# Graph layer plus masked attention in fp32: who makes the operand sums of the last two output projections, and when

## The chip, the cores and the metric

The kernel runs on one core of a Trainium2 chip. The metric is the device time of one execution in microseconds (us). A core has a matrix engine (TensorE, PE in the profile; its weight loads are PEld), VectorE (DVE), ScalarE (ACT), GpSimd (POOL) and SyncE (SP), whose queue issues DMA transfers. Each engine works through its own queue in program order and waits for the others through semaphores.

## The reference

Input x is 64 batches of 256 nodes with 512 features, with one 256x256 weighted adjacency for all of them. Two layers follow each other, each with a residual:

```python
h = relu(layernorm(x))
x = x + einsum('nm,bmd->bnd', adj, h) @ weight + bias
h = relu(layernorm(x))
q, k, v = h @ Wq + bq, h @ Wk + bk, h @ Wv + bv          # 8 heads of 64
scores = q @ k.T / 8 + (1 - adj) * -1e9                  # per head
x = x + softmax(scores) @ v  @ Wo + bo
```

All of it is fp32.

## The kernel before

**Groups.** The 64 batches are taken two at a time: 32 groups, g = 0 to 31 (`NG` = 32). Layer 0 runs over all groups first and leaves its results in DRAM; layer 1 then runs group after group. The output of the kernel is complete when the last group's output projection is added to its residual and sent out. Everything that the change touches lies in groups 30 and 31, so at the very end of the program.

**Projections with seven products.** A 512x512 projection (q, k, v, o) is split into halves in both directions and computed with seven products in place of eight (Strassen's scheme, in Winograd's form). That takes sums of weight blocks (`s1` to `s4`, made once) and sums of operand blocks, made for each group by `Halves.sums`, line 446: t1 = b12 - b11, t2 = b22 - t1, t3 = b22 - b12, t4 = b21 - t2. Each is one elementwise subtraction of 128x512. For the output projection the operand is `oT`, and its sums appear as `t_o` in the profile.

From group 2 on (`FIRST2`), `project2` splits three of the seven products once more. Their operand sums are made by `Blocks.sums` (lines 537 to 539), called through `block_outputs`: first from `oT` (tile `rest` for groups below 31, `t2o` for group 31), then from t4 (tile `t24o`).

`project2` is a generator with seven steps, written here with the tiles of the output projection of group g:

1. a11 x b11 into bank `o_ga`, added into the residual x
2. s3 x t3 into bank `o_gc`, added
3. s2 x t2 into `o_ga` again, added
4. the first small products of the three inner splits (one 128x128 product each), and `o_gb`
5. s1 x t1 into `o_ga`, added
6. the second small products of the inner splits (twelve matmul instructions), with six VectorE adds of 128x128
7. the rest: small products into `o_gc`, `o_ga`, the three third ones, the last adds, and the output DMA

Since `o_ga` is accumulated over several steps and read in between, step 3 waits until VectorE has added step 1's result, and step 5 until it has added step 3's. Both banks are seeded with the bias by ScalarE (`seeded`, line 255) before step 1.

**Attention.** A group's eight heads go in two halves, qd = 0 and 1. `score` computes the scores on TensorE (`sc`, 32 matmuls), VectorE scales and masks them (line 904), GpSimd subtracts a per-column maximum (line 910), ScalarE takes the exponential (line 915), and GpSimd adds the two key tiles (line 922, tile `as`). In group 31 the third of the four subtractions (by its place in the call order) is put on VectorE instead (line 908). `attend` multiplies `as` with ones for the denominators (`pden`) and the exponentials with v (`pav`), ScalarE copies the denominators out (line 947), VectorE inverts them (line 951, four pieces of 128x128; two of these before the next scores, two after, but all four at once for the last attention), and `divide` multiplies `pav` with the inverses into `oT` (line 969). Then it calls `note` (line 963: ScalarE sums the inverses into `stats`, for the overflow flag) and the operand sums described above.

**Order.** The program is written out by hand: the order in which Python issues the instructions is their order on each engine. `after(n, fn)` puts a call off by n ticks; `run(gen, n)` takes n steps of a generator, with a tick after each. So the engine that a sum runs on, and the tick at which it is issued, decide what stands before and behind it in a queue.

**Around the change.** For groups 30 and 31 the sums of `oT` are issued on VectorE, right inside `divide`. In group 31 the sums of the inner splits are on VectorE too, and `note` is called at once. After the scores of (31, 1), five steps of group 30's output projection run, then the last attention, then a tick (which brings its `divide`), then steps 6 and 7 of group 30, then six steps of group 31's projection, then the flag (lines 1078 to 1082: compare, reduce, a 1x1 matmul `pf`, copy), and step 7.

PSUM has eight banks, given out first-in first-out by `bank` and `give`. By that order, `o_30a` and `o_30c` are seeded into the banks that the third and the fourth VectorE mask operation (line 904) of the scores (31, 1) have emptied.

Of the kernel before, what the change touches and what calls it, by code (L numbers as in the profile page):

```python
# [198 lines left out]
def kernel(  # L199
# [16 lines left out]
    nc = tc.nc  # L216
# [7 lines left out]
    NG = B // GB  # L224
# [23 lines left out]
    def bank(shape, name, seed=None):  # L248

        i = next(i for i in free_banks if seed is None or whole[i])  # L250
        free_banks.remove(i)
        t = psum.tile(shape, F32, tag=f"bank{i}", name=name)
        bank_of[id(t)] = (i, t)
        if seed is not None:
            nc.scalar.copy(t, seed[:, None, :].to_broadcast(shape))
        return t

    def give(t, all_written=True):
        i = bank_of.pop(id(t))[0]
        free_banks.append(i)  # L260
        whole[i] = all_written
# [5 lines left out]
    def after(delay, fn, *args):  # L267
        entered[0] += 1
        later.append((clock[0] + delay, entered[0], fn, args))

    def tick():
        clock[0] += 1
        due = sorted((e for e in later if e[0] <= clock[0]), key=lambda e: e[:2])
        later[:] = [e for e in later if e[0] > clock[0]]
        for _, _, fn, args in due:
            fn(*args)
# [152 lines left out]
    class Halves:  # L429
# [12 lines left out]
        def sums(self, eng, which=("t1", "t2", "t3", "t4"), c=slice(0, 2)):  # L442
            args = {"t1": ("b12", "b11"), "t2": ("b22", "t1"), "t3": ("b22", "b12"), "t4": ("b21", "t2")}
            for n in which:
                p, q = args[n]
                eng.tensor_tensor(self.t[n][:, c, :], self.operand(p, c), self.operand(q, c), op=ALU.subtract)  # L446
# [61 lines left out]
    FIRST2 = 2  # L508
# [269 lines left out]
    H1T, HH, HO = {}, {}, {}  # L778

    def load_hidden(g):  # L780
        H1T[g] = xpool.tile([P, GB, DC, N], F32, tag="x", name=f"h1T_{g}")
        for k in range(GB):
            nc.sync.dma_start(H1T[g][:, k].rearrange("p d n -> p (d n)").rearrange("p (i n) -> p i n", n=N // NI),
                              HT[g][:, :, :, k, :].rearrange("p d i n -> p (d i) n"))

    def load_residual(g):
        X[g] = xpool.tile([P, T, D], F32, tag="x", name=f"x1_{g}")
        nc.sync.dma_start(X[g], X1[g].rearrange("k (t p) d -> p (k t) d", p=P))

    def hidden_sums(g, *steps):  # L790

        HH[g] = Halves(f"h_{g}", [H1T[g][:, k] for k in range(GB)], 0 if g else 1)
        for step, n in zip(steps, ("t3", "t1", "t2", "t4")):
            after(step, HH[g].sums, nc.gpsimd, (n,))
# [10 lines left out]
    def block_outputs(g, eng, step):  # L805
        x = OT[g][:, 2:4, :].rearrange("p c (k n j) -> p k c n j", k=GB, j=P)
        if g < NG - 1:
            t4 = act.tile([P, 4, P], F32, tag="t24o", name=f"t24o_{g}")
            t = AS["rest"][:, 2:4, :].rearrange("p k (q j) -> p k q j", j=P)
        else:  # L810
            t4 = act.tile([P, 4, P], F32, tag="t24", name=f"t24o_{g}")
            t = act.tile([P, GB, 4, P], F32, tag="t2", name=f"t2o_{g}")
        O2[g] = block_sums_of(x, t, HO[g], t4, eng, step)

    def block_sums_of(x, t, halves, t4, eng, step):
        both = Blocks(x, t)
        last = Blocks(halves.t["t4"].rearrange("p c (n j) -> p c n j", j=P), t4)
        after(step, both.sums, eng)
        after(step + 1, last.sums, eng)
        return {"b21": Blocks(x[:, 0], t[:, 0]), "b22": Blocks(x[:, 1], t[:, 1]), "t4": last}  # L820
# [40 lines left out]
    def seed_outputs(g):  # L861
        return seeded(L1["o"][1], f"o_{g}")
# [61 lines left out]
    def attend(g, qd):  # L924


        pd = bank([P, GN], f"pden_{g}_{qd}")
        po = [bank([P, GN], f"pav_{g}_{qd}_{f}") for f in range(2)]
        for b in range(GB):
            for h in range(4):  # L930
                nc.tensor.matmul(pd[h * 32:(h + 1) * 32, b * N:(b + 1) * N], ones[:, 0:32], AS[h // 2, b][:, h % 2, :],  # L931
                                 start=(b == 0), stop=True, tile_position=(0, h * 32), skip_group_check=True)
        for b in range(GB):
            v = V[g][qd, b]
            for k in range(NT):
                for f in range(2):
                    for h in range(4):
                        nc.tensor.matmul(po[f][h * 32:(h + 1) * 32, b * N:(b + 1) * N],  # L938
                                         v[:, k, h * HD + f * 32:h * HD + f * 32 + 32],
                                         A[h // 2, b][:, (h % 2) * NT + k, :],  # L940
                                         start=(b + k == 0), stop=(k == NT - 1), tile_position=(0, h * 32),
                                         skip_group_check=True)
        i = g * HQ + qd
        if i == 0:
            AS["rest"] = act.tile([P, 4, GN], F32, tag="yT1", name="rest")
        den, rden = AS["rest"][:, 0, :], AS["rest"][:, 1, :]
        nc.scalar.activation(den, pd, AF.Identity, accum_out=stats[:, 0, i:i + 1])  # L947
        give(pd)

        def invert(c):  # L950
            nc.vector.reciprocal(rden[:, c * P:(c + 1) * P], den[:, c * P:(c + 1) * P])  # L951

        early = 2 if g >= FIRST2 and (g, qd) != (NG - 1, 1) else 4
        for c in range(early):
            invert(c)
        if qd == 0:

            last = g == NG - 1
            OT[g] = (xpool if last else act).tile([P, DC, GN], F32, tag="x" if last else "r", name=f"oT_{g}")
            HO[g] = Halves(f"o_{g}", [OT[g][:, :, k * N:(k + 1) * N] for k in range(GB)], 0 if last else 1)  # L960

        def note():
            nc.scalar.activation(den, rden, AF.Identity, accum_out=stats[:, 1, i:i + 1])

        def divide():
            for c in range(early, 4):
                invert(c)
            for f in range(2):
                nc.vector.tensor_tensor(OT[g][:, 2 * qd + f, :], po[f], rden, op=ALU.mult)
                give(po[f])  # L970
            if g < NG - 1:
                after(3, note)
            else:
                note()
            eng = nc.gpsimd if g < NG - 2 else nc.vector
            if qd == 0:
                HO[g].sums(eng, ("t1",))
            else:
                HO[g].sums(eng, ("t3", "t2", "t4"))
                if g >= FIRST2:  # L980
                    block_outputs(g, eng if g == NG - 1 else nc.gpsimd, 8 if g == NG - 2 else 2)

        after(1, divide)

    def run(gen, steps=99):

        for _ in zip(range(steps), gen):
            tick()
# [50 lines left out]
    for g in range(NG):  # L1039
        attend(g, 0)  # L1040
        load_residual(g)
        if g + 2 < NG:
            load_hidden(g + 2)
        score(g, 1, 5 if g < NG - 1 else 3)
        tick()
        if g == 0:
            for n, tag in ((4 * DC, "w0_sb"), (4, "w0_s1"), (4, "w0_s2"), (4, "w0_s4"), (4, "adjT"), (4, "b0_r")):
                t = const.tile([P, n, P], F32, tag=tag, name=f"spare_{tag}")
                spare.extend(t[:, i, :] for i in range(n))
        for n, at in (("q", 7),) if g == 0 else (("k", 1), ("v", 5)) if g == 1 else (("o", 2),) if g == 2 else ():  # L1050
            for i, work in enumerate(block_sums(n)):
                after(at + i // 3, *work)
        if g + 1 < NG:
            run(queries_keys(g + 1))
        else:
            last = post(g - 1, seed_outputs(g - 1))
            run(last, 5)
        attend(g, 1)
        if g + 1 < NG:
            score(g + 1, 0, 5)  # L1060
            tick()
            steps = values(g + 1)
            run(steps, 5)
            seeds = seed_outputs(g) if g + 2 < NG else None
            run(steps)
            if g + 2 < NG:
                hidden_sums(g + 2, 2, 3, 4, 5)
                if g + 2 >= FIRST2:
                    block_hidden(g + 2, 6)
                run(post(g, seeds))  # L1070
    tick()
    run(last)
    last = post(NG - 1, seed_outputs(NG - 1))
    run(last, 6)

    bad = tmp.tile([P, 2 * NG * HQ], F32, tag="u", name="bad")
    worst = small.tile([P, 1], F32, tag="worst", name="worst", bufs=1)
# [41 lines left out]
```

## Time and profile before

| what | value |
|---|---|
| median of 8 runs | 2678.29 us (2676.13 to 2680.62) |
| the profiled execution | 2680.57 us, of which the span is 2678.7 us |
| PE, PEld busy in the span | 2646.5 us (99%), 2281.4 us (85%) |
| DVE, ACT, POOL busy | 1860.0 us (69%), 965.5 us (36%), 1779.5 us (66%) |
| scores of (31, 1) start on PE | 2623.12 us |
| output projection of group 30 starts | 2632.26 us |
| last attention (`pden`) starts | 2643.32 us |
| output projection of group 31 starts | 2654.43 us |
| last PE and last DVE instruction end | 2671.8 and 2672.3 us |

The profiled execution is one run, 2.3 us above the median. Times inside it count from the span's start. The table of windows gives, for each stretch, its length, the busy time of PE, PEld, DVE, ACT and POOL with the number of instructions, the mean TensorE clock as a share of the full one, the DMA share and GB/s. The timeline lists start, duration, engine, line, output and inputs, and in square brackets how long the engine had been idle and whose work ended that.

### The profile page before, as it was taken

To read this page: it belongs to the slowest core of one execution; us is meant where nothing else is said; L and a number is where in the kernel's file an instruction comes from. 1 tells how busy PE (TensorE), PEld (TensorE's weight loads), DVE (VectorE), ACT (ScalarE), POOL (GpSimd) and SP (SyncE) were. 2 spreads that over 40 slices of the span, in tenths; PEclk is the share of its full clock that TensorE was granted. 3 is DMA by queue.
4 is the path that set the end of the run, shared out by engine and by line. 5 is a ranking of instruction groups with operands and counts; after the bars stand their busy time and mean duration, and the time that the engine had idled before them with its cause. 6 is when DMAs were issued, how large, how long until landed. Compare 5 with 4: busy or idle time off the path is not lost.

```text
span 2678.7 us, 50183 instructions
## 1 busy us (share of the span) xinstructions
PE 2646.5 (99%) x19332; PEld 2281.4 (85%) x19332; DVE 1860.0 (69%) x4103; ACT 965.5 (36%) x1875; POOL 1779.5 (66%) x1568
## 2 busy tenths in 40 slices
PE   8999999999999999999999999999999999999997
PEld 7888888888888888888888888888888888888885
DVE  7777777774467666667676666676766666667676
ACT  4444445453333333333333333333333333333331
POOL 3454544444778777777777777777777777777772
PEclk9999999999999999999999999999999999999998
DMA  7776666663122211111111111122221111111110
GB/s 185 185 198 168 157 171 165 171 160 80 47 64 57 55 48 48 48 48 48 48 49 48 48 48 48 48 56 65 65 54 48 48 48 48 49 48 48 48 48 33
DMA packets 281058, 210.93 MB, mean 79 GB/s; under 512 B 145904, under 2 KB 212976, under 8 KB 280816
## 3 DMA queue, kind: packets, MB, share of 16 engines
q1 hardware_dynamic: 280352, 207.15, 29.8%
q8 instruction: 155, 2.54, 0.4%
q14 instruction: 87, 0.71, 0.1%
q10 hardware_dynamic: 464, 0.52, 0.1%
HBM read 106.96 MB, written 100.66 MB: 78 GB/s over the span
## 4 chain that ended last, share of the span: by engine, by line
PE 97%; DVE 2%; DMA 0%; ACT 0%; issue 0%; POOL 0%; ACTq 0%; DVEq 0%
PE sc L898 9%; PE pav L938 8%; PE py L714 8%; PE q L564 3%; PE k L564 3%; PE v L564 3%; PE o L564 3%; PE pden L931 2%; DVE a L904 0%; DVE x L665 0%; PE o_30a L453 0%; PE w_1a L453 0%; PE v_1a L453 0%; PE q_1a L453 0%; PE w_31a L453 0%; PE w_22a L453 0%
## 5 line engine op out<-in xcount | busy, mean ns | idle before, releaser
L910 POOL TENSOR_TENSOR a<-a,top 128x1024 f32<-128x1024 f32 x254 | 592.5, 2366 | 493.9 <-DVE a L904 493.9
L904 DVE SCALAR_TENSOR_TENSOR a<-sc,maskT 128x512 f32<-128x512 f32 x512 | 312.0, 682 | 121.9 <-PE sc L898 121.9
L922 POOL TENSOR_TENSOR as<-a 128x512 f32<-128x512 f32 x256 | 318.9, 1278 | 9.1 <-ACT a L915 8.0
L915 ACT ACTIVATE a<-a 128x1024 f32<-128x1024 f32 x256 | 270.6, 1058 | 10.2 <-POOL a L910 7.8
L53 POOL TENSOR_TENSOR rs<-rs,mhalf 128x2 f32<-128x2 f32 (+1 forms) x97 | 77.9, 803 | 267.6 <-DVE nb L52 267.5
L951 DVE RECIPROCAL rest<-rest 128x128 f32<-128x128 f32 x256 | 224.5, 920 | 34.4 <-ACT rest L947 34.4
L898 PE MATMUL sc<-q,k 64*128 64x256 f32 x2048 | 238.4, 382 | 0.0
L938 PE MATMUL pav<-a,v 128*32 128x256 f32 x4096 | 233.6, 379 | 0.0
L898 PEld LDWEIGHTS sc<-q,k 64*128 64x128 f32 x2048 | 194.2, 187 | 44.7 <-issue 26.3
L714 PE MATMUL py<-adjT,h 128*128 128x256 f32 x1024 | 228.6, 382 | 0.9 <-DVE adjT L333 0.9
L714 PEld LDWEIGHTS py<-adjT,h 128*128 128x128 f32 x1024 | 196.0, 192 | 28.6 <-ACT h L693 1.2
L938 PEld LDWEIGHTS pav<-a,v 128*32 128x32 f32 x4096 | 133.4, 110 | 87.9
L741 ACT ACTIVATE h<-x,nb,rs 128x512 f32<-128x512 f32 x128 | 97.1, 806 | 307.1 <-POOL nb L54 307.1
L947 ACT ACTIVATE rest<-pden 128x512 f32<-128x512 f32 x64 | 38.3, 598 | 414.7 <-PE pden L931 414.7
L665 DVE TENSOR_TENSOR k<-k,k 128x128 f32<-128x128 f32 (+1 forms) x300 | 96.2, 353 | 126.0 <-PE k L564 124.0
L446 POOL TENSOR_TENSOR t_y<-yT 128x256 f32<-128x256 f32 (+1 forms) x96 | 87.5, 912 | 46.0 <-ACT yT L724 42.5
L665 DVE TENSOR_TENSOR x<-o,x 128x128 f32<-128x128 f32 (+1 forms) x360 | 111.1, 350 | 3.1
L665 DVE TENSOR_TENSOR q<-q,q 128x128 f32<-128x128 f32 (+1 forms) x300 | 96.1, 353 | 13.5 <-PE q L564 11.4
L665 DVE TENSOR_TENSOR v<-v,v 128x128 f32<-128x128 f32 (+1 forms) x300 | 95.4, 352 | 14.5 <-PE v L564 11.4
L761 DVE BATCH_NORM_STATS2 st<-x 128x6 f32<-128x256 f32 x256 | 96.4, 419 | 4.4
L693 ACT ACTIVATE h<-x,nb,rs 128x512 f32<-128x512 f32 x128 | 93.9, 806 | 9.7 <-POOL nb L54 9.7
L446 POOL TENSOR_TENSOR t_y<-yT,t_y 128x256 f32<-128x256 f32 (+1 forms) x96 | 87.3, 917 | 13.1 <-ACT yT L724 13.1
(4280 smaller groups left out, 6499.4 us busy)
## 6 DMA issues: line engine op xcount, KB each, us to landing
x<-in_x_dram SPq DMA_DIRECT2D x256, 128.0 KB, 3.3
residual<-x SPq DMA_DIRECT2D x256, 128.0 KB, 2.3
hidden<-r SPq DMA_DIRECT2D x128, 256.0 KB, 4.5
h1T<-hidden SPq DMA_DIRECT2D x64, 512.0 KB, 9.7
x<-residual SPq DMA_DIRECT2D x32, 1024.0 KB, 7.5
out_dram<-x SPq DMA_DIRECT2D x62, 512.0 KB, 4.1
w_sb<-in_L_gnn_weight_dram SPq DMA_DIRECT2D x1, 1024.0 KB, 8.9
wq_sb<-in_L_gnn_Wq_dram SPq DMA_DIRECT2D x1, 1024.0 KB, 6.3
```

What stands on the lines that cost most here:

```text
L446: eng.tensor_tensor(self.t[n][:, c, :], self.operand(p, c), self.operand(q, c), op=ALU.subtract)
L564: nc.tensor.matmul(o[:, 0, :], lhs, rhs, start=start, stop=True, skip_group_check=True)
L665: nc.vector.tensor_tensor(o, ps, u, op=ALU.add)
L714: nc.tensor.matmul(pss[d][:, b * N:(b + 1) * N], h[:, b * NT + k, d * P:(d + 1) * P], adjT[:, k, :], start=(b + k == 0), stop=(k == NT - 1 ...
L741: nc.scalar.activation(h1[:, k * NT + t, :], xt[:, k * NT + t, :], AF.Relu, bias=nb[:, t:t + 1], scale=rs[:, t:t + 1])
L898: nc.tensor.matmul(ps[j][:, kt * N:(kt + 1) * N], k[j * HD:(j + 1) * HD, c, kt * P:(kt + 1) * P], q[j * HD:(j + 1) * HD, c, :], start=(kt ...
L904: nc.vector.scalar_tensor_tensor(a[:, j * NT:(j + 1) * NT, :].rearrange("p k n -> p (k n)"), ps[j], SCALE, maskT_f, op0=ALU.mult, op1=ALU.add)
L910: nc.gpsimd.tensor_tensor(a, a, top_b, op=ALU.subtract)
L915: nc.scalar.activation(a, a, AF.Exp)
L922: nc.gpsimd.tensor_tensor(AS[c, b], a4[:, :, 0, :], a4[:, :, 1, :], op=ALU.add)
L938: nc.tensor.matmul(po[f][h * 32:(h + 1) * 32, b * N:(b + 1) * N], v[:, k, h * HD + f * 32:h * HD + f * 32 + 32], A[h // 2, b][:, (h % 2) * ...
L951: nc.vector.reciprocal(rden[:, c * P:(c + 1) * P], den[:, c * P:(c + 1) * P])
```

## The change

For groups 30 and 31 all sums of `oT` go to GpSimd, as they already do for groups 0 to 29. For (30, 1) they are issued seven ticks later (`wait`), with the inner sums at ticks 8 and 9 as before; for (30, 0), (31, 0) and (31, 1) they are issued inside `divide` as before, and the inner sums of group 31 one and two ticks later in place of two and three. In group 31 `note` is put off too: by three ticks for (31, 0), by two for (31, 1). Step 6 of group 30's output projection is issued ahead of the last attention. The tick after that attention is gone, so its `divide` is issued after step 7 of group 30. The flag is computed after step 2 of group 31's projection in place of step 6.

```diff
             for f in range(2):
                 nc.vector.tensor_tensor(OT[g][:, 2 * qd + f, :], po[f], rden, op=ALU.mult)
                 give(po[f])
-            if g < NG - 1:
-                after(3, note)
+            after(2 if (g, qd) == (NG - 1, 1) else 3, note)
+            wait = 7 if (g, qd) == (NG - 2, 1) else 0
+            sums = lambda: HO[g].sums(nc.gpsimd, ("t3", "t2", "t4") if qd else ("t1",))
+            if wait:
+                after(wait, sums)
             else:
-                note()
-            eng = nc.gpsimd if g < NG - 2 else nc.vector
-            if qd == 0:
-                HO[g].sums(eng, ("t1",))
-            else:
-                HO[g].sums(eng, ("t3", "t2", "t4"))
-                if g >= FIRST2:
-                    block_outputs(g, eng if g == NG - 1 else nc.gpsimd, 8 if g == NG - 2 else 2)
+                sums()
+            if qd and g >= FIRST2:
+                block_outputs(g, nc.gpsimd, wait + 1 if g >= NG - 2 else 2)
...
             last = post(g - 1, seed_outputs(g - 1))
-            run(last, 5)
+            run(last, 6)
         attend(g, 1)
...
-    tick()
     run(last)
     last = post(NG - 1, seed_outputs(NG - 1))
-    run(last, 6)
+    run(last, 2)
```

In the queues this gives the following order. On GpSimd, t3, t2 and t4 of group 30 stand between the `as` sums of (31, 0) and the subtractions of (31, 1); t1 of group 31 stands between the inner sums of group 30; the remaining nine sums of group 31 stand at the end. On VectorE, the four inversions of the last attention stand behind step 6's adds, and the two multiplications into `oT` behind all adds of step 7. On ScalarE, the two bias seeds of group 30 no longer stand behind `note` of (31, 0). On SP, the load of the flag stands ahead of all four output transfers of group 31, where it stood behind the first.

## The prediction

> **What bounds the kernel now.** The page's chain of work comes first: PE carries 97% of it, so a change counts only where it closes a gap on PE, or makes one.
>
> ```profile
> PE 97%; DVE 2%; DMA 0%; ACT 0%; issue 0%; POOL 0%; ACTq 0%; DVEq 0%
> ```
>
> The change touches the last 80 us alone. There I read PE's timeline for gaps (brackets: idle time and who ended it):
>
> ```profile
> 2612.26 0.49 PE L564 MATMUL v<-spare_w_s,t 128*128 128x128 f32 x2 [3.87 <-DVE v L665]
> ...
> 2632.26 3.78 PE L453 MATMUL o_30a<-wo_sb,oT 128*128 128x256 f32 x8 [5.41 <-ACT o_30a L255]
> ...
> 2652.79 0.49 PE L564 MATMUL o<-spare_w_s,rest 128*128 128x128 f32 x2 [2.07 <-DVE x L665]
> ...
> 2667.82 0.19 PE L1081 MATMUL pf<-ones,worst 128*1 128x1 f32 x2 [1.96 <-DVE worst L1079]
> ```
>
> Four gaps, 13.3 us, each ended by VectorE or by ScalarE behind it. Then the table of windows, in stretches of 3.4 us, for what the gaps do to the clock (column after POOL's count):
>
> ```profile
> 2610.20:2613.60 3.40, 1.34 (x12) 1.35 (x13) 3.40 (x6) 0.00 (x0) 0.72 (x1) 1.00 0.00 0
> 2613.60:2617.00 3.40, 3.40 (x19) 3.40 (x18) 2.21 (x8) 0.94 (x4) 0.00 (x0) 0.51 0.00 0
> ...
> 2630.70:2634.10 3.40, 1.84 (x4) 1.51 (x5) 2.52 (x4) 3.10 (x6) 3.40 (x2) 0.51 0.00 0
> 2634.10:2637.50 3.40, 3.40 (x9) 2.70 (x8) 1.37 (x2) 1.50 (x2) 3.17 (x5) 0.50 0.00 0
> ...
> 2654.60:2658.00 3.40, 3.40 (x9) 2.69 (x9) 3.18 (x9) 0.00 (x0) 0.00 (x0) 0.51 0.34 129
> ...
> 2668.20:2671.60 3.40, 3.40 (x18) 3.35 (x17) 1.69 (x4) 0.00 (x0) 0.00 (x0) 0.52 0.02 5
> ```
>
> Every gap is followed by PE work at half clock, which costs half its busy time: 1.7 + 0.9 + 1.7 + 1.7 + 1.7 = 7.7 us more. Last, why VectorE is late at the first gap (timelines of DVE and POOL):
>
> ```profile
> 2606.36 3.44 DVE L446 TENSOR_TENSOR t_o<-oT,t_o 128x512 f32<-128x512 f32 x2
> 2609.72 2.28 DVE L908 TENSOR_TENSOR a<-a,top 128x1024 f32<-128x1024 f32 x1
> ```
> ```profile
> 2605.85 5.07 POOL L922 TENSOR_TENSOR as<-a 128x512 f32<-128x512 f32 x3
> ```
>
> The same two t_o take 1.41 us at 2650.66, where GpSimd is idle, and the other L908 takes 1.22; three `as` sums should take 3.8 (row of page part 5: 1278 ns each). Both engines are slow while they meet.
>
> [...] It matters as much that adds from PSUM (L665) should not block: at 2578.03 four `as` sums take 4.97 us, full speed, beside running L665 adds. [...]
>
> **The change, step by step** (times on the span's clock of before; "lead" is before minus after).
>
> 1. *t1 of (30, 0), and t3, t2, t4 of (30, 1), leave VectorE.* The first had PE running on through both sides, and goes to GpSimd ahead of `as` sums that end at 2583 and are wanted at 2591.8: nothing, with 7.5 us of cover for 1.3 (without it, 1.3). Without the other three, `oT` ends at 2605.3, L908 waits for GpSimd's subtraction (to 2605.9), takes 1.22, and the first v add is done at 2607.3. PE is ready at 2608.2: the 3.87 gap goes, and with it the half-clock stretch. The small v products end at 2611.6 in place of 2617.4. New is who is late next: the last exponential sits on ScalarE behind the copy of `v_31a`; copy, exponential and `as` sum took 2616.45 to 2619.11 = 2.66 after PE's part. That part now ends at 2611.06, so `pden` finishes from 2613.7. Lead 5.4.
>
> 2. *`note` of (31, 0) no longer stands ahead of the seeds.* `note` waited until 2630.99 for inversions behind eight masks. The seeds' banks are emptied by masks 3 and 4. Masks start at 2624.4 - 5.4 - 0.2 = 2618.8; the third ends 1.8 later, seed 0.5: `o_30a` can start at 2621.1, just as the scores end. The 5.41 gap and its slow clock go. Steps 1 and 2 take 3.5 in place of 6.2, to 2624.6.
>
> 3. *A new wait.* Step 3 needs step 1's add, which on VectorE stands behind all masks (to 2623.6), two inversions (1.75) and `oT` (1.3), plus 0.6: 2627.1. PE stands 2.5 us; lead 11.3, probably with one slow stretch (up to 1.7).
>
> 4. *GpSimd becomes the bound of the last attention.* From the second mask on: three subtractions 2619.9 to 2626.8 (3 x 2.32), then inner sums of `rest` 1.3 + 0.75 + 0.75, one L908 in between (1.2), t1 of group 31 1.3, inner sums of `t24o` 0.75 + 0.5 + 0.45, four `as` 4.95: 2638.8. Step 6 is done by about 2635 (its twelve products and six adds hide in this wait, so that half of step 3's loss costs nothing), and PE waits some 4 us for `as`. Before, the last `as` ended at 2643.7. Lead 5.0. The three t_o on GpSimd (3.9 us, 2613.7 to 2617.6) fit in its wait for the first masks.
>
> 5. *Step 6 was ahead, `divide` comes after.* `pav` 3.5, up to 0.9 for the clock, step 7's products 2.0: 2645.6. Before, four inversions, `oT` and three t_o on VectorE held up step 6's adds: the 2.07 gap (2.4 with two small ones) and 1.7 of half clock go. `o_31a` needs only t and seeds that are ready; before it started at 2654.4. Lead 8.8.
>
> 6. *What is behind on VectorE and GpSimd.* VectorE's inversions (2640.3 to 2643.7) now hold the adds of step 7, which end at 2646.8; `oT` 1.3 to 2648.1; t3 on GpSimd 1.3. `o_31c` starts at 2649.5 in place of 2657.6: PE stands 2.1. Lead 8.1.
>
> 7. *The flag earlier.* `pf` stands behind `o_31c` (1.9 with its tail) and waits for an add (0.6), compare and reduce (0.55): 2652.7, a gap of 1.4. Before, the gap came behind step 6, was 1.96, and half clock followed it (1.7). Step 3 of group 31 starts at 2652.8 in place of 2659.6: lead 6.8. On SP the flag's load now waits ahead of the first output transfer; that one's data come at about 2658.4, so nothing.
>
> 8. *To the end.* Products of steps 3 to 7 at full clock: 1.73 + 0.67 + 0.67 + 1.73 + 1.34 + 1.34 + 0.67 = 8.15, to 2661.0. VectorE becomes the later one: behind step 5's add (to 2658.4) six adds take 2.05, two 0.6 each, three 0.36 each: with their waits 2662.6, in place of 2672.3. The last output transfer and the end, 6.4 us, stay. GpSimd's nine sums take 8.9 from 2648.2 to about 2657; the last wanted ones (t24o) are wanted at 2657.6 and later.
>
> Sum: 9.6 us. Against the profiled run, 2680.57 - 9.6 = 2671.0; it stands 2.3 above the median, so the median becomes 2678.29 - 9.6 = **2668.7**.
>
> Unknown sizes. [...] a slow one at steps 5 to 8 more costs 1.7, one less gives 1.0 back; two of each at most. Meetings of L908 and sums: 0 to 2.4, I took 1.2. GpSimd's sums later than their rows, in points 4 and 6: up to 2. So the gain lies between 6 and 12.5.
>
> **Rivals.** *A, GpSimd costs more than its row says.* If step 1's stall shrinks by half only (an L908[...], 1.3, and a slow window kept, 1.7), GpSimd's queue in step 4 moves back by 3, and with t24o late by 1 to 2 for step 6 of group 31's projection, the gain is 3 to 6: 9.6 - 3 - 1.5 = 5.1, or 2673.2. For it: VectorE and GpSimd already meet there. Against: only one VectorE operation of two SBUF inputs is left in each stretch. *B, slower.* VectorE's adds from PSUM block GpSimd too, so each of the 11 sums and subtractions of point 4 and the nine of point 8 waits 0.9 us (what a t_o lost at 2606): 20 x 0.9 - 1.8 (slack at the end) = 16.2 against 9.6, slower by 6.6: 2684.9. It decides from 0.6 us a sum on. Against it stands the 4.97 above. *C, the seeds do not get free* (they wait for `oT`, to 2626.5 + 0.5): `o_30a` then starts 6 later and at half clock, but the waits of points 3 and 4, 2.5 + 4, hide all but about 1; gain 8.5, 2669.8. The stall removed is then worth nearly nothing either way.
>
> **How the numbers follow.** The case of the sum has 0.78, with C in it 0.80; A 0.15, B 0.05. About 0.2% (5.4 us) is what a measurement of this kernel can tell from no change. The first case is faster by more; A is mostly within it; B slower. Faster 0.83, same 0.12, slower 0.05. The range reaches from 12.5 + some run-to-run spread below, 2664.5, to A's 2674.5.
>
> **What would show it.** Right: no gap ahead of the small v products at about 2608 and none ahead of `o_30a`; a new gap of 2 to 3 us ahead of step 3 of group 30, ended by VectorE; a wait of `pden` for `as`, 3 to 5 us in sum; `o_31c` waiting for t_o of GpSimd, 2 us; `pf` 1.4 us; the nine last sums at 1.28 us per 128x512. Wrong: `as` or t_o rows well above 1.3 us beside L665 (B); v products still waiting over 2 us (A); a part of the trace before 2570 us that differs.

## The result, and the profile after

The changed kernel takes 2671.15 us (median of 12 runs, 2670.28 to 2672.80), the kernel before 2679.12 us (32 runs, 2676.13 to 2681.77). The ratio is 0.9972, 95% interval 0.9964 to 0.9979: by the ratio 7.5 us faster, between 5.6 and 9.6 (the two medians differ by 8.0). The forecast was faster, 2668.7 us, range 2664.5 to 2674.5.

The table of waits of the changed kernel, PE alone, from 2597 us to the end (total, times, longest in us):

```profile
PE pden L931 <- POOL as L922: 3.2, 3, 1.6
PE o_30a L453 <- DVE x L665: 2.3, 1, 2.3
PE pf L1078 <- DVE worst L1076: 2.3, 1, 2.3
PE o_31c L453 <- POOL t_o L446: 1.9, 1, 1.9
```

The same table of the kernel before has five lines: `o_30a` for its seed 5.4 us, the small v products 3.9, the third small products 2.4 (in three waits), `pf` 2.0 and `pden` 0.6. The first three are gone, the waits of step 3 (second line) and of `o_31c` are new, `pden` waits longer, and `pf` waits at another place. GpSimd now ends two of the four. In sum PE stands 9.7 us in place of 14.3.

The two profiled executions reach this stretch at slightly different times. As common origin I take the start of the scores (31, 0) on PE, ahead of which PE has the same instructions in both. Before:

```profile
2596.22 3.72 PE L898 MATMUL sc<-q,k 64*128 64x256 f32 x32
```

After, PE's timeline:

```profile
2596.94 3.72 PE L898 MATMUL sc<-q,k 64*128 64x256 f32 x32
...
2614.44 0.41 PE L931 MATMUL pden<-as,ones 128*32 128x256 f32 x2 [1.00 <-POOL as L922]
...
2628.30 3.43 PE L453 MATMUL o_30a<-wo_s,t_o 128*128 128x256 f32 x8 [2.33 <-DVE x L665]
...
2639.71 0.41 PE L931 MATMUL pden<-as,ones 128*32 128x256 f32 x2 [0.59 <-POOL as L922]
...
2645.83 1.89 PE L453 MATMUL o_31a<-wo_sb,oT 128*128 128x256 f32 x8
2649.64 1.99 PE L453 MATMUL o_31c<-wo_sb,t_o 128*128 128x256 f32 x8 [1.92 <-POOL t_o L446]
2653.92 0.19 PE L1078 MATMUL pf<-ones,worst 128*1 128x1 f32 x2 [2.29 <-DVE worst L1076]
```

From the origin, in us (the forecast's points, with 2596.22 taken off):

| event | before | forecast | after |
|---|---|---|---|
| last `pden` part of (31, 0) starts | 22.9 | 17.5 | 17.5 |
| `o_30a` starts | 36.0 | 24.9 | 25.3 |
| step 3 of group 30 starts | 42.2 | 30.9 | 31.4 |
| last `as` of (31, 1) ends on GpSimd | 47.5 | 42.6 | 42.7 |
| `o_31a` starts | 58.2 | 49.4 | 48.9 |
| `o_31c` starts | 61.4 | 53.3 | 52.7 |
| step 3 of group 31 starts | 63.4 | 56.6 | 57.1 |
| VectorE's last add ends | 76.1 | 66.4 | 67.0 |
| end of the span | 82.5 | 72.8 | 72.3 |

GpSimd took its sums at the durations that were counted on, beside VectorE's adds from PSUM (timeline of POOL, changed kernel):

```profile
2634.71 4.95 POOL L922 TENSOR_TENSOR as<-a 128x512 f32<-128x512 f32 x4
...
2648.32 1.26 POOL L446 TENSOR_TENSOR t_o<-oT 128x512 f32<-128x512 f32 x1 [8.66 <-DVE oT L969]
2649.55 2.61 POOL L446 TENSOR_TENSOR t_o<-oT,t_o 128x512 f32<-128x512 f32 x2
```

Of the stretches at half clock one is left ahead of the end of the span, behind the new wait of step 3 (windows table, the clock is the column after POOL's count; the stretch lies across two windows, and from 2629.5 to 2631.7 us the clock is 0.50):

```profile
2627.30:2630.70 3.40, 2.40 (x7) 1.96 (x8) 3.40 (x4) 1.50 (x4) 3.32 (x3) 0.70 0.00 0
2630.70:2634.10 3.40, 3.40 (x20) 3.12 (x19) 2.18 (x7) 0.76 (x1) 3.24 (x5) 0.80 0.00 0
```

Even this one cost nothing here. The kernel with the flag undone (below) has the same instructions up to step 2 of group 31's projection. In its trace step 3 of group 30 took 1.97 us in place of 3.43, after the same wait of 2.33, `pden` then waited 4.0 us in sum for `as` in place of 3.2, and `o_31a` started 48.9 us from the origin, as above.

### The profile page after: what moved, and what is told of

Same layout as the page of the kernel before. It is cut to its first block, busy times and chain, and to the rows that moved or that the text cites. A ratio compares the mean times of both kernels' runs of the same rounds, so it can differ in the third digit from the quotient of the medians.

```text
span 2669.2 us, 50186 instructions
## 1 busy us (share of the span) xinstructions
PE 2641.4 (99%) x19332; PEld 2276.5 (85%) x19332; DVE 1848.8 (69%) x4089; ACT 965.3 (36%) x1875; POOL 1795.1 (67%) x1582
## 5 line engine op out<-in xcount | busy, mean ns | idle before, releaser
L665 DVE TENSOR_TENSOR k<-k,k 128x128 f32<-128x128 f32 (+1 forms) x300 | 96.1, 353 | 126.1 <-PE k L564 124.0
L446 POOL TENSOR_TENSOR t_y<-yT 128x256 f32<-128x256 f32 (+1 forms) x96 | 87.8, 915 | 45.9 <-ACT yT L724 42.6
L665 DVE TENSOR_TENSOR x<-o,x 128x128 f32<-128x128 f32 (+1 forms) x360 | 111.0, 350 | 3.1
L665 DVE TENSOR_TENSOR q<-q,q 128x128 f32<-128x128 f32 (+1 forms) x300 | 96.1, 353 | 13.8 <-PE q L564 11.7
L665 DVE TENSOR_TENSOR v<-v,v 128x128 f32<-128x128 f32 (+1 forms) x300 | 95.4, 352 | 14.5 <-PE v L564 11.4
```

The lines of the kernel that those rows point to most:

```text
L665: nc.vector.tensor_tensor(o, ps, u, op=ALU.add)
```

## The experiments

Each kernel is given by its edit against the kernel before or the changed kernel. "From the origin" is its span after the start of the scores (31, 0): 82.5 before, 72.3 changed.

The experiments ran in three later series, each beside new runs of the kernel before, whose medians were 2679.12 to 2679.92 us; the changed kernel was not run again. The ratio, to the kernel before of the same series, is therefore what is compared, and a microsecond between two medians of different series means little. Single executions differ too, in two places that the change does not touch: the origin lies anywhere from 2595.12 to 2597.22 us in the fourteen traces, and the stretch from VectorE's last add to the end of the span takes 5.0 to 5.3 us in eleven of them, but 6.4 in the kernel before, 6.2 with the flag undone and 6.8 with fillers in the kernel before. No run shows why. Where this matters, the end of VectorE's last add is given beside the end of the span: 76.1 us from the origin before, 67.0 changed.

### Which part carries the gain: the sums alone, note alone

The first takes only the sums of the change:

```diff
-            eng = nc.gpsimd if g < NG - 2 else nc.vector
-            if qd == 0:
...
+            wait = 7 if (g, qd) == (NG - 2, 1) else 0
+            sums = lambda: HO[g].sums(nc.gpsimd, ("t3", "t2", "t4") if qd else ("t1",))
...
```

> The kernel before with one part of the change: the sums of groups 30 and 31 on GpSimd, those of (30, 1) seven ticks later. Theory: the v gap goes, so GpSimd reaches the last as sums about 4 earlier (at 2639.7 on the clock of the trace before); note still holds the seeds, but that wait hides in the wait for as; nearly the whole gain of the change, 5 to 8 us: 2671 to 2674. Rival (the parts add up, each gap is its own gain): 3 to 4 us only, 2675 to 2676.

Measured: 2669.85 us (6 runs, 2669.40 to 2670.81), ratio 0.9964 (0.9951 to 0.9977); 72.3 from the origin (last add 67.0). One part of four gives the whole gain. Its waits on PE:

```profile
PE o_30a L453 <- ACT o_30a L255: 5.4, 1, 5.4
PE pden L931 <- POOL as L922: 2.1, 3, 1.0
PE pf L1082 <- DVE worst L1080: 2.0, 1, 2.0
PE o L564 <- DVE x L665: 0.3, 2, 0.2
```

The 5.4 us gap ahead of `o_30a` is still there in full, and costs nothing: PE still comes to `pden` before GpSimd is done. The 2.07 gap at the third small products is gone as well, without step 6 being moved: what had held up its adds were the three t_o on VectorE.

The second takes only the later `note`:

```diff
-            if g < NG - 1:
-                after(3, note)
-            else:
-                note()
+            after(2 if (g, qd) == (NG - 1, 1) else 3, note)
```

> The kernel before with one part of the change: note of group 31 called later. Theory: the 5.41 gap ahead of o_30a shrinks to nothing, then step 3 waits for VectorE, and pden waits for as sums that GpSimd ends no earlier (about 2643.7): 0 gained, and up to 1.7 lost if pav falls into a half-clock stretch: 2678 to 2681. Rival (gap of its own): 5 to 8 us faster, 2671 to 2674.

Measured: 2679.71 us (12 runs, 2678.50 to 2682.04), ratio 1.0000 (0.9991 to 1.0009). The largest gap of the profile before was removed and nothing was gained; VectorE's last add ends 76.0 from the origin in place of 76.1. PE waits for VectorE ahead of step 3 and longer for `as` instead, beside the three other waits of before:

```profile
PE o_30a L453 <- DVE x L665: 3.4, 1, 3.4
PE pden L931 <- POOL as L922: 1.6, 2, 1.0
```

### Undoing one part at a time

The sums back on VectorE (the first diff of this section in reverse, in the changed kernel):

> The changed kernel with the sums of groups 30 and 31 on VectorE again. Theory: the 3.9 gap at the small v products and its half clock come back (scores 5.4 later than in the changed kernel); GpSimd has t1 less to do, so pden ends about 4 later; at the end t3 takes 0.7 in place of 1.3 and compare runs undisturbed, -1.5: 2.5 us slower than the changed kernel, about 2673.7 (2672.5 to 2675.5). Rival (GpSimd is simply slower at sums, and the gain came from the order): 1 us or more faster than the changed kernel.

Measured: 2678.56 us (20 runs, 2675.01 to 2680.42), ratio 0.9994 (0.9988 to 1.0001); 81.4 from the origin in the trace, which is of the slowest of the 20 runs. By the ratios it is about 6 us slower than the changed kernel, against 2.5 expected, and not told apart from the kernel before: the other three parts, kept here, bring nothing clear without the sums. So the rival falls and the theory had its size wrong. Its three longest waits:

```profile
PE v L564 <- DVE v L665: 3.9, 1, 3.9
PE o_30a L453 <- DVE x L665: 3.3, 1, 3.3
PE pf L1077 <- DVE worst L1075: 2.9, 1, 2.9
```

The last `pden` part comes 48.7 after the origin in place of 42.8 (six later, not four: the v products ran at half clock again, 0.63 us a pair in place of 0.39, and from the first small one to the start of `pden` it took 6.1 us in place of 3.4), and step 3 of group 31 stands behind a longer `pf` wait, because the sums of `t2o` sit ahead of the compare on VectorE, and then runs at half clock too (3.78 for eight matmuls in place of 1.99).

`note` at once again:

```diff
-            after(2 if (g, qd) == (NG - 1, 1) else 3, note)
+            if g < NG - 1:
+                after(3, note)
+            else:
+                note()
```

> The changed kernel with note called at once in group 31, as before. Theory (GpSimd bounds the last attention): the seeds of o_30a stand behind note again, o_30a starts about 5 us later and steps 1 and 2 run at half clock, but PE then reaches pden at about 2639.7 on the changed kernel's clock, just when the last as sum lands there, so 0 to 1 us slower than the changed kernel: 2671 to 2672.5. Rival (the 5.41 gap ahead of o_30a is gain of its own): 5 to 8 us slower than the changed kernel, 2676 to 2679.

Measured: 2671.85 us (8 runs, 2670.54 to 2672.25), ratio 0.9970 (0.9959 to 0.9981); 72.3 from the origin, as the changed kernel (the trace is of the fastest of the eight runs). The gap ahead of `o_30a` is back with 5.41 us; the wait of `pden` for `as` falls from 3.2 to 1.0, and step 3's 2.3 are gone. It is the forecast's rival C in a stronger form: no cost shows at all.

Step 6 behind the last attention again, and the tick:

```diff
-            run(last, 6)
+            run(last, 5)
...
+    tick()
     run(last)
```

> The changed kernel with step 6 of group 30 behind the last attention again and the tick (so divide ahead of steps 6 and 7). Theory: step 6's products cost 1.3 again and its adds wait behind inversions and oT (gap of about 2 at the third small products), but oT is done 2.3 earlier, so the 1.92 wait of o_31c for t3 on GpSimd goes: within 1 us of the changed kernel, 2670.5 to 2672.5. Rival (step 6 ahead is a gain of its own, as points 4 and 5 of the prediction count it): 3 to 4 us slower, 2674 to 2675.

Measured: 2670.92 us (6 runs, 2670.42 to 2671.17), ratio 0.9970 (0.9957 to 0.9982): no different by the times. Its trace ends 73.5 from the origin, 1.2 later than the changed kernel (last add 68.3 in place of 67.0). In it the wait of `o_31c` is gone and that for `as` is 4.8 in place of 3.2, as the theory has it; no gap appears at the third small products, where I had expected 2.

The flag after step 6 of group 31 again:

```diff
-    run(last, 2)
+    run(last, 6)
```

> The changed kernel with the flag computed after step 6 of group 31 again. Theory: the 2.29 gap of pf ahead of step 3 goes, step 4 waits some 0.7 for t2o on GpSimd instead, and a gap of about 2 comes back ahead of pf at the end, with a half-clock stretch after it worth up to 1.7: 0 to 2 us slower, 2671 to 2673. Rival (the flag is better late, where GpSimd no longer disturbs compare): 1 to 2 us faster, about 2669.5.

Measured: 2671.03 us (6 runs, 2670.53 to 2672.67), ratio 0.9970 (0.9957 to 0.9982): no different. The `pf` wait is 1.9 at the end in place of 2.3 earlier, and step 4 waits 0.6 for t2o. The last add ends 67.3 from the origin (67.0 in the changed kernel).

So three of the four parts are worth nothing that these times can tell, each taken away by itself (step 6 with the tick some 1 us by the traces), and the fourth gives everything by itself.

### The seven ticks

```diff
-            if wait:
-                after(wait, sums)
-            else:
-                sums()
+            sums()
```

> The changed kernel with t3, t2 and t4 of (30, 1) on GpSimd at once in place of seven ticks later, so ahead of the as sums of (31, 0). Theory (what matters is that they leave VectorE; the delay only keeps them out of the way of as): the last as of (31, 0) ends 1.2 later, and everything behind it: 2672.3 (2671.5 to 2673.5). Rival (the delay is the gain): the v gap or an equal one at pden comes back, 3 to 5 us slower, 2674.5 to 2676.

Measured: 2675.24 us (20 runs, 2674.41 to 2678.68), ratio 0.9986 (0.9980 to 0.9993): about half of the gain is lost. The size is the rival's; of its mechanism no gap comes back at the v products, but a longer wait appears at `pden`. GpSimd's timeline shows the three sums ahead of `as`:

```profile
2605.60 2.26 POOL L446 TENSOR_TENSOR t_o<-oT 128x512 f32<-128x512 f32 x1
2607.82 2.63 POOL L446 TENSOR_TENSOR t_o<-oT,t_o 128x512 f32<-128x512 f32 x2
2610.41 4.95 POOL L922 TENSOR_TENSOR as<-a 128x512 f32<-128x512 f32 x4
```

The first takes 2.26 us, since L908 on VectorE (1.73) falls on it, and the first `as` ends so late that `pden` of (31, 0) waits 2.7 in place of 1.0. That puts the scores (31, 1) 1.9 later from the origin, where the theory had 1.2. The span ends 5.2 later. The rest lies in two stretches at half clock (granted clock 0.57 in the windows 2640.92 to 2644.34 and 2657.99 to 2661.40) whose loss no later wait takes up: `o_31a` is 3.5 later (the last 62 matmuls of `pav` took 5.17 in place of 3.83), VectorE's last add 5.2 later (step 3 of group 31 took 2.90 for eight matmuls in place of 1.99, and the small products behind it 0.63 each in place of 0.39). Whether the delay brings these two stretches, or they fell there by chance in this execution, one trace does not show; its time, 2675.20, is that of the median.

### Half clock

Matmuls whose results nobody reads, in two gaps of the kernel before:

```diff
+    def fill(n, name):
+        t = bank([P, GN], name)
+        for i in range(n):
+            nc.tensor.matmul(t[:, 0:N], ident, maskT[:, i % NT, :], start=True, stop=True, skip_group_check=True)
+        give(t)
...
+        if name == f"o_{NG - 2}":
+            fill(5, "fill_u3")
         for p, c in zip(inner, ((0, 0), (1, 0), (0, 1))):
...
+    fill(4, "fill_pf")
     pf = bank([1, 1], "pf")
```

> The kernel before with nothing of the change, but with matmuls whose result nobody reads in two gaps: five 128x256 ones ahead of the third small products of group 30 (gap 2.07) and four ahead of pf (gap 1.96). Theory (the half-clock stretches after these gaps are a loss of their own, 1.7 us each): the stretches at o_31a and after pf go, 2 to 3.4 us faster: 2675 to 2677. Rival (only the waits count, or fillers delay what waits): no change or slower by up to 1, 2678 to 2680.

Measured: 2678.56 us (12 runs, 2676.32 to 2680.29), ratio 0.9996 (0.9987 to 1.0005). The times alone leave it open (from 3.5 us faster to 1.3 slower). The trace shows that the stretches at half clock go, and are worth less than I expected: `o_31a` and `o_31c` now run at full clock,

```profile
2654.23 1.89 PE L459 MATMUL o_31a<-wo_sb,oT 128*128 128x256 f32 x8
2655.95 1.89 PE L459 MATMUL o_31c<-wo_sb,t_o 128*128 128x256 f32 x8
2658.21 1.99 PE L459 MATMUL o_31a<-wo_s,t_o 128*128 128x256 f32 x8 [0.36 <-DVE x L673]
```

where the first took 3.38 before, and the small products behind `pf` take 0.39 in place of 0.63; but step 3 then waits for VectorE. VectorE's last add ends 1.8 earlier from the origin (74.3) and the span 1.4 earlier (81.1), not 2 to 3.4. With one trace of each kernel this is no measured gain.

The same in the changed kernel's four waits:

```diff
+        if (g, qd) == (NG - 1, 1):
+            fill(4, "fill_d")
         pd = bank([P, GN], f"pden_{g}_{qd}")
...
+        if name == f"o_{NG - 1}":
+            fill(3, "fill_c")
         product(pc, s, "s3", halves, "t3", by_token, start=not seeds, stop=False)
...
+        if name == f"o_{NG - 2}":
+            fill(4, "fill_a")
         product(pa, s, "s2", halves, "t2", by_token, start=False, stop=False)
...
+    fill(4, "fill_pf")
     pf = bank([1, 1], "pf")
```

> The changed kernel with matmuls whose result nobody reads in its four waits: four 128x256 ahead of step 3 of group 30, four ahead of pden, three ahead of o_31c, four ahead of pf (0.43 us each). Theory (what is left of half clock in the changed kernel is hidden in the waits for VectorE and GpSimd, apart from single runs): the half-clock stretch at step 3 goes, but pden still waits for as: within 1 us of the changed kernel, 2670.3 to 2671.5, with the upper runs near 2672.5 gone. Rival (half clock accounts for the two microseconds that the forecast had too much): 2 us faster, 2669.

Measured: 2669.73 us (5 runs, 2669.66 to 2670.58), ratio 0.9967 (0.9953 to 0.9980); 72.3 from the origin, as without (last add 67.0 in both), as the theory has it, though the median lies 0.6 below the theory's range. The changed kernel's 12 runs fall into six from 2670.28 to 2670.89, one at 2671.40 and five from 2672.22 to 2672.80; here none of five lies in the upper part. That fits a half-clock stretch that in some runs falls where PE is not waiting anyway, but the six runs with step 6 undone all lie below 2671.2 without fillers, and the traces show one run of each kernel, so it is not shown.

### What a better order gives

The tick alone put back (step 6 stays ahead of the attention):

```diff
+    tick()
     run(last)
```

> The changed kernel with the tick kept after the last attention, so that divide (oT) stands ahead of step 7's adds on VectorE; step 6 stays ahead of the attention. Theory: oT is done about 2645.8 in place of 2648.3 on the changed kernel's clock, t3 on GpSimd 1.3 later, and the 1.92 wait of o_31c goes: about 2 us faster than the changed kernel, 2669.2. Rival (step 7's adds behind oT hold the seed of o_31c or step 3): 0 to 1 us slower.

Measured: 2668.38 us (5 runs, 2667.61 to 2670.38), ratio 0.9960 (0.9945 to 0.9975); 70.3 from the origin, 2.0 less than the changed kernel (the intervals of the two ratios overlap). The wait of `o_31c` for t3 is gone. So by the traces moving step 6 brings 3.2 us where the tick stays (73.5 to 70.3), and the removal of the tick takes 2.0 of them back.

With the 1x1 matmul of the flag two steps later than its compare and reduce as well:

```diff
+    run(last, 2)
     pf = bank([1, 1], "pf")
```

> The changed kernel with the tick kept and the 1x1 matmul of the flag issued two steps after its compare and reduce; t1 stays where the change put it. Theory: 1.2 us less than with the tick alone (2668.4): 2667.2, and 1.2 us more than the kernel with t1 put off too. Rival: no difference from the tick alone.

Measured: 2666.18 us (4 runs, 2665.25 to 2668.41), ratio 0.9954 (0.9939 to 0.9970); 68.4 from the origin, 1.9 less than with the tick alone, where 1.2 was expected. And with t1 of (31, 0) behind the last `as` sums:

```diff
-            wait = 7 if (g, qd) == (NG - 2, 1) else 0
+            wait = 7 if (g, qd) in ((NG - 2, 1), (NG - 1, 0)) else 0
```

> The changed kernel with three edits: the tick kept after the last attention (as in the kernel with the tick kept, 2668.4 us), the 1x1 matmul of the flag issued two steps after its compare and reduce, so that PE need not wait for them, and t1 of (31, 0) put off by seven ticks, behind the last as sums. Theory: the pf gap (1.8) goes, of which some 0.6 comes back as a wait of step 4 for t2o on GpSimd, and the wait of pden for as shrinks by t1's 1.27: 2666 (2665 to 2667.5). Rival (GpSimd's nine last sums are the bound of the tail): 2668, as with the tick alone.

Measured: 2665.30 us (5 runs, 2664.76 to 2665.58), ratio 0.9948 (0.9935 to 0.9962); 67.0 from the origin, so 1.3 less again in the trace, t1's own length; the intervals of the last three overlap, so the steps between them rest on the traces. The median is 5.8 us below that of the changed kernel, beside the same median of the kernel before (2679.12), and the intervals of these two ratios do not overlap. Its waits on PE:

```profile
PE pden L931 <- POOL as L922: 2.9, 3, 1.3
PE o_30a L453 <- DVE x L665: 2.3, 1, 2.3
PE o_31b L564 <- POOL t2o L539: 0.5, 1, 0.5
PE o_30b L564 <- POOL rest L539: 0.4, 1, 0.4
```

## Why the prediction was right, and where not

**The verdict and the mechanism held.** Of the eight points, 1 to 4 came within 0.5 us from the origin. With the sums back on VectorE the 3.9 us gap is back. That alone would also fit a queue that is merely longer; the durations tell the two apart (the kernel with the sums back, two t_o beside GpSimd's `as` sums, and two with GpSimd idle):

```profile
2607.36 3.43 DVE L446 TENSOR_TENSOR t_o<-oT,t_o 128x512 f32<-128x512 f32 x2
2655.12 1.41 DVE L446 TENSOR_TENSOR t_o<-oT,t_o 128x512 f32<-128x512 f32 x2
```

In the trace of before, the three t_o and L908 take 6.8 us in sum at this place and 3.3 undisturbed, so by estimate some 3.5 us of the gap are this slowing. The adds from PSUM did not hold GpSimd up (1.26 us for a t_o, 4.95 for four `as`), so rival B's mechanism does not show here. Its sum was off besides: point 4 lists fourteen GpSimd instructions, not eleven, which would have made B slower by 9.3 us in place of 6.6. Rival A did not come either: L908 took 1.74 and 2.30 us in the two stretches, 1.6 more than twice 1.22, where 1.2 had been set aside.

**Point 4 was the point that matters.** GpSimd's chain up to the last `as` ended 0.1 us from where it was put, with some luck: the subtractions ended 0.5 later than forecast, and the meeting with L908 cost less than the 1.2 counted. PE's wait for it was 2.2 us, not some 4, since PE came later, step 3 having run at half clock. Since the chain ends later than PE's own work, everything that only brings PE there sooner is worth nothing. That was said of the seeds (rival C, with a cost of 1.1); the measured one is nil in both directions.

**Points 5 to 7 had the times right and the credit wrong.** They let the lead grow from 5.0 to 8.8 by moving step 6 and dropping the tick. The sums alone reach the same end (72.3 from the origin). The gap at the third small products belonged to the t_o on VectorE, so it goes with the sums; and dropping the tick made the wait of `o_31c` (1.9) that took back 2.0 of the 3.2 us that step 6 saves in the traces. The forecast had this wait, at 2.1, without asking whether the old order would do better.

**Point 7 was mis-sized.** The `pf` wait was 2.3 in place of 1.4. The compare was counted at 0.22 us, as before; it took 1.11:

```profile
2652.35 1.11 DVE L1075 TENSOR_SCALAR bad<-stats 128x128 f32<-128x128 f32 x1
```

With the flag at the end, where GpSimd is idle (the kernel with that undone), it is short again:

```profile
2658.85 0.22 DVE L1075 TENSOR_SCALAR bad<-stats 128x128 f32<-128x128 f32 x1
```

It has one SBUF input, and I had counted only operations with two as slowed, as the trace of before shows them (t_o and L908, above); there two inversions of 128x128, with one input, took 1.75 us beside GpSimd's subtractions (at 2602.25) and 1.76 with GpSimd idle (at 2620.57). In the trace of the changed kernel the compare ends 0.09 us after the GpSimd sum that was running when it started (2652.11 to 2653.37). No run shows why the compare is slowed and the inversions are not.

**The step from the profile to the median was the one that failed.** The sum against the profiled run gave 2671.0, and the changed kernel's profiled run took 2671.08. That run of before stood 2.3 above the median then known, 1.45 above the one of 32 runs; the changed kernel's stands at its own median (2671.08 and 2671.15). I carried the excess over as if both kernels had it. It belonged to that execution, and the traces show where most of it lay: the end behind VectorE's last add took 6.4 us there and 5.0 to 5.3 in most others. The kernel with the later `note` alone, whose last add comes at the same place and whose trace stands at its median, ends 81.3 from the origin in place of 82.5. Point 8 had let the 6.4 us stay; the changed kernel took 5.2. So the exact agreement with 2671.0 has luck in it: VectorE's last add came 9.0 us earlier from the origin, where 9.7 was forecast, the end took 1.2 less, and the way to the origin 0.7 more. Why the kernel before spreads over 5.6 us (2676.13 to 2681.77) and the changed one over 2.5 stays open; four gaps with half clock behind each may give more room for it than one such stretch hidden in a wait, and the fillers don't settle it.

## What to carry to other kernels

The longest gap on the bounding engine need not be the one to close first: ask what the work behind it waits for next, and close the chain that ends last there. A sum that goes to another engine is worth what it frees on the one that holds others up (here 5.4 us at the first `pden`, for three subtractions that undisturbed take 1.3 us each in place of 0.7), provided it stands behind the work that others wait for in its new queue: without the seven ticks half of the gain was lost. When a step is moved ahead of a wait that hides it, check what else the move pushed back.

## What the runs showed of the hardware

- A one-input compare of 128x128 on VectorE takes 0.22 us with GpSimd idle and 0.60 to 1.11 us beside GpSimd's sums (0.60 with the tick kept, 0.73 with step 6 undone, 1.02 with `pf` two steps later, 1.11 in the changed kernel). In the changed kernel it ends 0.09 us after a GpSimd sum ends, and in the other three about 0.1 after one, by estimate from the end of `oT`, with GpSimd's sums laid out behind it as in the changed kernel; so its length fits what was left of that sum. An add of 128x512 with one input in PSUM and one in SBUF (L665) took 0.69 us just ahead of it in all four.
- The same wait is not always followed by half clock. After 2.33 us ahead of step 3 of group 30, its eight matmuls took 3.43 us in the trace of the changed kernel, and 1.96 or 1.97 in the five with step 6 undone, the flag undone, the tick kept, and the two better orders built on it.
- The half-clock stretch that fell ahead of a wait cost nothing (step 3 of group 30 took 3.43 us in the changed kernel and 1.97 with the flag undone, `o_31a` started at 48.9 in both). With the sums at once, two such stretches on unhidden work took 3.2 us on top of a delay of 1.9.
